# Output biases of a routed feed-forward layer: from a matrix product at the end to rows gathered per expert and added at the evacuation

## The chip, the core and the metric

The kernel runs on one core of a Trainium2 chip. Times are device microseconds (us) of one execution on that core. Engines: PE is TensorE's matmul, PEld its weight load, DVE is VectorE, ACT is ScalarE, POOL is GpSimd, SP is SyncE, which only issues transfers here. POOL issues every indirect transfer (rows picked by a list of numbers) and some plain ones.

## What is computed

There are 625 tokens of width 1024. A layer norm and a relational graph convolution come first (20000 edges, two kinds, 286 hidden columns, ELU, product with `wo`), then a second layer norm and a feed-forward part with two shared experts and two of eight routed experts for each token:

```python
sh = gelu(einsum('td,sdh->sth', xf, sW1) + sb1)          # 2 shared experts
shared = (einsum('sth,shd->std', sh, sW2) + sb2).mean(0)
topk_vals, topk_idx = top_k(xf @ rW + rb, 2)
probs = softmax(topk_vals)                               # two weights that sum to 1
y = einsum('eth,ehd->etd', gelu(einsum('td,edh->eth', xf, W1) + b1), W2) + b2
out = x + shared + sum over the two chosen experts of probs * y
```

The change concerns the two biases of the second products, `sb2` (2 x 1024) and `b2` (8 x 1024).

## The kernel before

Tokens lie in NT = 5 tiles of TP = 125. The kernel is one straight program, `sparse_kernel`; a framework puts each engine's instructions in an order and adds the waits, and a tile of a pool is handed out again when its last user is through. `tc.issue_after(x)` places an instruction behind `x`. A second, dense kernel stands behind a flag and is not entered here.

The stages, in order of PE:

1. Counting and projection (up to 88 us). Edges become one-hot columns `ohs` and `ohk` on DVE (the last instruction on `ohs` is L850), PE counts them (`cnt`), and between these it forms the projections `p_pr` (L891). POOL starts with constants and small loads, among them those of `bd`, a DRAM table of both biases three times over (L625, L627).
2. Aggregation and output product of the graph part (`p_agg`, `p_y`, up to 134 us), with the second layer norm; rows of the norm go to DRAM as `h2d`, those of the residual as `x1d`.
3. Routing (134 to 170 us). `gate` forms the gates, `route` the two weights `w`, `slots` gives every token-expert pair a place. There are NJ = 11 routed tiles of 128 places; a tile is one expert's, or is shared by two of 64 places or four of 32. In `slots` DVE makes one-hots `oh` and `oj` (L1242 to L1246), a product of them on PE gives `p_tok` (L1250), and DVE reads from it `tok` (which token a place holds) and `row` (where in DRAM its result goes). PE fills the time with the shared experts' first product, `shared_in` (`p_sh`, L1137), whose calls are written out between these steps. Then `weights_T` splits the weights into three bfloat16 parts, transposes them on PE (`p_wT`, L1298) into `wT`, and `bias_parts` loads `bd` three times into `b2x` (L635) and splits it into `b23` (L639, L640, L642).
4. Routed experts, first product (170 to 221 us). `fetch` gathers the tokens of a tile from `h2d` into a tile `xs` of the pool `io`, which has three buffers (L1332); PE transposes them (`p_x`), multiplies (`p_h`, L1359) and transposes back (`p_hT`).
5. Routed experts, second product (221 to 260 us). For every tile of `ORDER` PE makes two halves `p_yj` of 128x512 (L1417) in five PSUM banks; the halves are copied to a tile `ys` of the pool `gat` (15 buffers of 4 KB a partition) by DVE (L1421), from the fifth tile on every first half by ACT (L1423). POOL then scatters the 128 rows to the DRAM table `yt` (L1425). `gat` also holds copies `w2m` of weights for the shared tiles (12 of them, made by ACT, L1408) and later the gathered rows `gs`.
6. Output (260 us to the end). PE makes the shared experts' second product `p_o`: for each of 11 column groups eight float32 matmuls (L1472), and one of bfloat16, `wT` against `b23`, which adds all biases (L1474). SP loads the result rows of both choices of each token, `gs`, from `yt` (L1436) once the scatters have landed. DVE adds in a fixed order (L1448): half of `p_o` to `x1` for a group, and each `gs` times its weight; the rows of the last three token tiles are added in one block ahead of their `p_o`. Then the output is stored.

The place the biases have in this:

```python
                nc.tensor.matmul(p[:TP, :n], wT[:, own], b23[:, at], start=False, stop=True)
            add(x1[:, d, at], p[:TP, :n], 1.0 / NS, x1[:, d, at])
```

Of the kernel before, what the change touches and what calls it, by code (L numbers as in the profile page):

```python
# [8 lines left out]
F32 = mybir.dt.float32  # L9
# [8 lines left out]
N = 625  # L18
# [434 lines left out]
def sparse_kernel(  # L453
# [166 lines left out]
    for i in (2, 3):  # L620
        nc.gpsimd.tensor_add(join, join, ident[:, QC * i : QC * (i + 1)])


    bd = dram.tile([3, NS + NE, D], F32, name="bd")
    nc.gpsimd.dma_start(bd[:, :NS, :], bass.AP(tensor=sb2.tensor, offset=sb2.offset,  # L625
                                               ap=[[0, 3], [D, NS], [1, D]]))
    nc.gpsimd.dma_start(bd[:, NS:, :], bass.AP(tensor=b2.tensor, offset=b2.offset,  # L627
                                               ap=[[0, 3], [D, NE], [1, D]]))
    b23 = const.tile([3 * QC, D], BF16, name="b23")

    def bias_parts():
        b2x = io.tile([3 * QC, D], F32, tag="io", name="b2x")
        nc.vector.memset(b2x, 0.0)
        for j in range(3):
            nc.gpsimd.dma_start(b2x[j * QC : j * QC + 3 * (NS + NE)], bd.rearrange("i e d -> (i e) d"))  # L635
        b2h = rt.tile([3 * QC, D], BF16, name="b2h")
        for j in range(3):
            with tc.issue_after(named.ins):
                nc.vector.tensor_copy(b2h, b2x)  # L639
            nc.scalar.copy(b23[j * QC : (j + 1) * QC], b2h[j * QC : (j + 1) * QC])  # L640
            if j < 2:
                nc.vector.tensor_sub(b2x, b2x, b2h)  # L642

# [180 lines left out]
    nc.vector.memset(nil, 0.0)  # L824
    MAXG = max(GROUPS)
    ends = [R * TP * min(DB * (b + 1), NT) for b in range((NT + DB - 1) // DB)]

    def count_windows(between):
        accs = []
        c0 = 0  # L830
        for g in GROUPS:
# [17 lines left out]
            nc.vector.tensor_tensor(os, row[:, None].to_broadcast(shape), key, op=ALU.is_equal)  # L849
            nc.vector.tensor_tensor(os, os, both(VV_, 128)[1], op=ALU.mult)  # L850
            shape, key = both(KW_, KR)
# [148 lines left out]
    at(50, clear)  # L1000
    at(30, transpose_vec)
    at(6, scales, 0, 2)
    at(18, scales, 2, 4)
# [93 lines left out]
    w = const.tile([TP, NT, NS + NE], F32, name="w")  # L1097
    wT = hid.tile([3 * QC, N], BF16, name="wT")
    sel = const.tile([TP, NT, NE], F16, name="sel")
    wide = [TP, NT, NE]  # L1100

    def route():
        full = [TP, NT, NE, NE]
        other = gates[:, :, None, :].to_broadcast(full)
        own = gates[:, :, :, None].to_broadcast(full)
        nc.vector.tensor_scalar(lower, lower, 0.0, None, op0=ALU.is_gt)
        above = rt.tile(full, F32, name="above")
        equal = rt.tile(full, F32, name="equal")
        nc.vector.tensor_tensor(above, other, own, op=ALU.is_gt)
        nc.vector.tensor_tensor(equal, other, own, op=ALU.is_equal)  # L1110
        nc.vector.tensor_mul(equal, equal, lower[:, None, :, :].to_broadcast(full))
        nc.vector.tensor_add(above, above, equal)
        cnt = const.tile(wide, F32, name="cnt")
        nc.vector.tensor_reduce(cnt, above, axis=AX.X, op=ALU.add)
        nc.vector.tensor_scalar(sel, cnt, 1.5, None, op0=ALU.is_lt)
        top = const.tile([TP, NT], F32, name="top")
        nc.vector.tensor_reduce(top, gates, axis=AX.X, op=ALU.max)
        ex = const.tile(wide, F32, name="ex")
        nc.vector.tensor_sub(ex, gates, top[:, :, None].to_broadcast(wide))
        nc.scalar.activation(ex, ex, AF.Exp)  # L1120
        nc.vector.tensor_mul(ex, ex, sel)
        tot = const.tile([TP, NT], F32, name="tot")
        nc.vector.tensor_reduce(tot, ex, axis=AX.X, op=ALU.add)
        inv = const.tile([TP, NT], F32, name="tot_inv")
        nc.vector.reciprocal(inv, tot)
        nc.vector.memset(w[:, :, :NS], 1.0)
        nc.vector.tensor_mul(w[:, :, NS:], ex, inv[:, :, None].to_broadcast(wide))
# [18 lines left out]
    tok = const.tile([128, NJ], I32, name="tok")  # L1146
    row = const.tile([128, NJ], I32, name="row")
    ej = const.tile([1, nt + 4], I32, name="ej")

    def slots():  # L1150
# [64 lines left out]
        both_ = [TP, 2, NT, NE]  # L1215
        nc.vector.tensor_tensor(m, m, ab[:, :, :, None].to_broadcast(both_), op=ALU.is_equal)
        nc.vector.tensor_mul(m, m, w[:, None, :, NS:].to_broadcast(both_))
        nc.vector.tensor_reduce(wab, m, axis=AX.X, op=ALU.add)
# [19 lines left out]
        oh = rt.tile([TP, 2, NT, 128], F16, name="oh")  # L1238
        oj = const.tile([TP, 2, NT, NJ], F16, name="oj")
        q = ps_mm("p_tok")  # L1240
        for a in range(2):
            nc.vector.tensor_tensor(oh[:, a], it[:, None, :].to_broadcast([TP, NT, 128]),  # L1242
                                    pc[:, 0, a][:, :, None].to_broadcast([TP, NT, 128]), op=ALU.is_equal)
            nc.vector.tensor_tensor(oj[:, a], it[:, None, :NJ].to_broadcast([TP, NT, NJ]),
                                    pc[:, 1, a][:, :, None].to_broadcast([TP, NT, NJ]), op=ALU.is_equal)
            nc.vector.tensor_mul(oj[:, a], oj[:, a], tid[:, a, :, None].to_broadcast([TP, NT, NJ]))  # L1246
        shared_in(0, 1)
        for a in range(2):
            for t in range(NT):
                nc.tensor.matmul(q[:, :NJ], oh[:, a, t], oj[:, a, t],  # L1250
                                 start=(a == 0 and t == 0), stop=(a == 1 and t == NT - 1))
# [3 lines left out]
        nc.vector.scalar_tensor_tensor(t[:, 1], q[:, :NJ], -1.0, t[:, 0], op0=ALU.add, op1=ALU.subtract)  # L1255
        named = nc.vector.tensor_scalar(tok, t[:, 1], 0.0, float(N - 1), op0=ALU.max, op1=ALU.min)
        nc.vector.tensor_scalar(t[:, 0], q[:, :NJ], 0.5, 4.0 * YB, op0=ALU.is_lt, op1=ALU.mult)
        nc.vector.tensor_tensor(row, t[:, 0], q[:, :NJ], op=ALU.add)

        for at in (0, NH2):  # L1260
# [18 lines left out]
        nc.vector.tensor_tensor(flag, flagf[:, 0:1], flagf[:, 1:2], op=ALU.add)  # L1279
        return named  # L1280

    def weights_T():
        nc.vector.tensor_scalar(w[:, :, NS:], w[:, :, NS:], float(NS), None, op0=ALU.mult)
        NW_ = NS + NE
        part = rt.tile([TP, NT, 3 * QC], F32, name="part")
        nc.vector.memset(part, 0.0)
        near = const.tile([TP, NT, NW_], BF16, name="near")
        for i in range(3):
            nc.vector.tensor_copy(near, w)
            for j in range(3):  # L1290
                at = j * QC + i * NW_
                nc.vector.tensor_copy(part[:, :, at : at + NW_], near)
            if i < 2:
                nc.vector.tensor_sub(w, w, near)
        for a, b in ((0, 3), (3, NT)):
            p = ps_mm(f"p_wT_{a}")
            for d in range(a, b):
                nc.tensor.transpose(p[: 3 * QC, (d - a) * TP : (d - a + 1) * TP], part[:, d, :],  # L1298
                                    ident[:TP, :TP])
            nc.vector.tensor_copy(wT[:, a * TP : b * TP], p[: 3 * QC, : (b - a) * TP])  # L1300

    gate()
    route()
    named = slots()
    weights_T()
    bias_parts()
    for t in range(HK):
# [92 lines left out]
    gat = pool(ctx, "gat", 15, side="right")  # L1400

    ORDER = (*whole[:3], *range(NM2), *whole[3:])
    w2m = {}
    for j in ORDER:
        for a, _, e in parts(j)[1:]:
            for k in range(HK):
                w2m[j, a, k] = gat.tile([128, D], F32, tag="y", name=f"w2m_{j}_{a}_{k}")
                nc.scalar.copy(w2m[j, a, k][:, None, :], w2a[:, bass.ds(e, 1), k, :])  # L1408
    sent = []
    for n, j in enumerate(ORDER):  # L1410
        y = gat.tile([128, D], F32, tag="y", name=f"ys_{j}")
        for s in range(2):
            at = slice(s * 512, (s + 1) * 512)
            p = ps_acc(f"p_yj_{j}_{s}")
            for k in range(HK):
                for a, b, e in parts(j):
                    made = nc.tensor.matmul(p[a:b], hjT[:, j, k, a:b],  # L1417
                                     w2m[j, a, k][:, at] if a else w2a[:, bass.ds(e, 1), k, at],
                                     start=(k == 0), stop=(k == HK - 1))
            if s or n < 4:  # L1420
                nc.vector.tensor_copy(y[:, at], p)  # L1421
            else:
                nc.scalar.copy(y[:, at], p)  # L1423

        sent.append(nc.gpsimd.indirect_dma_start(  # L1425
            out=yt, out_offset=bass.IndirectOffsetOnAxis(ap=row[:, j : j + 1], axis=0), in_=y, in_offset=None,
            bounds_check=2 * YB - 1, oob_is_err=False))
        for s in sent[:-1]:
            tc.declare_no_dep(sent[-1].ins, s.ins, reason="rows of different slots")

    gs = {}
# [27 lines left out]
    for d in range(NT):  # L1459
# [4 lines left out]
        for at in ((0, 512), (512, D)) if d < NT - 1 else ((0, 512), (512, 768), (768, D)):  # L1464
# [4 lines left out]
            with tc.issue_after(made.ins):  # L1469
                for i in range(NS):  # L1470
                    for k in range(HK):
                        nc.tensor.matmul(p[:TP, :n], shT[:, i, k, own], sw2[:, i, k, at],  # L1472
                                         start=(i == 0 and k == 0), stop=False)
                nc.tensor.matmul(p[:TP, :n], wT[:, own], b23[:, at], start=False, stop=True)  # L1474
            add(x1[:, d, at], p[:TP, :n], 1.0 / NS, x1[:, d, at])
# [47 lines left out]
```

## Time and profile before

| what | us |
|---|---|
| median of 3 runs (lowest, highest) | 304.88 (304.16, 305.06) |
| the profiled execution, its own time | 303.7 |
| its span in the trace | 301.4 |
| PE busy | 290.8 (96%) |
| DVE busy | 168.4 (56%) |
| ACT busy | 107.5 (36%) |
| POOL busy | 45.2 (15%) |

The trace covers 301.4 us of an execution that took 303.7 us; the 2.3 us around it belong to start and end. The granted TensorE clock was 0.997 of full speed. Sums made from the trace are differences against 301.4 or 303.7, and the same difference is then set against the median. A row of the groups gives busy time, mean nanoseconds of one instruction, and the idle time before it with what ended it; the chain gives, in order of time, the start, the length, the engine and the line of each piece of work that set the end.

### The profile page before, as it was taken

What the parts mean: (1) busy time and instruction counts of PE and PEld (TensorE: products, weight loads), DVE (VectorE), ACT (ScalarE), POOL (GpSimd) and SP (SyncE); (2) the same over time, 40 slices, a digit from 0 to 9 for tenths busy, and PEclk for the clock granted to TensorE, in tenths of its full rate; (3) what the DMA queues carried; (4) which work ended last, traced back from release to release, by engine and by line L of the source; (5) the groups of instructions that cost most, each with busy time, mean ns of one, the idle gap of its engine ahead of it and who ended that gap; (6) DMA issues with size and microseconds to landing.
All of it is one profiled execution on the core that took longest, in us unless ns stands there. A gap on an engine that the chain in (4) does not pass through costs nothing.

```text
span 301.4 us, 4682 instructions
## 1 busy us (share of the span) xinstructions
PE 290.8 (96%) x1649; PEld 194.9 (65%) x1649; DVE 168.4 (56%) x465; ACT 107.5 (36%) x246; POOL 45.2 (15%) x98
## 2 busy tenths in 40 slices
PE   8799999999999799999999999999999999999993
PEld 6687777787889534376777887887843334444452
DVE  5999999998327668756883122212223211255921
ACT  2455118355334432155123244638359311000000
POOL 9500000000000014240131212210003222200000
PEclk9999999999999999999999999999999999999998
DMA  7999910000009999965999253340057555479442
GB/s 243 304 318 393 421 65 2 0 2 1 0 17 340 348 348 391 400 195 182 348 396 410 86 203 96 114 141 3 0 190 276 221 209 210 191 291 385 161 138 73
DMA packets 27408, 61.15 MB, mean 203 GB/s; under 512 B 2176, under 2 KB 16007, under 8 KB 27375
## 3 DMA queue, kind: packets, MB, share of 16 engines
q1 hardware_dynamic: 21806, 43.77, 40.7%
q0 software_dynamic: 5280, 16.69, 15.7%
q10 hardware_dynamic: 294, 0.35, 0.5%
q8 instruction: 15, 0.25, 0.3%
q14 instruction: 13, 0.10, 0.1%
HBM read 42.76 MB, written 18.81 MB: 204 GB/s over the span
## 4 chain that ended last, share of the span: by engine, by line
PE 93%; DVE 4%; ACT 1%; issue 0%; ACTq 0%
PE p_pr L891 20%; PE p_h L1359 13%; PE p_yj L1417 13%; PE p_o L1472 11%; PE p_sh L1137 10%; PE p_y L952 6%; PE p_agg L909 6%; PE p_x L1340 3%; PE p_t L795 3%; PE cnt L868 2%; PE p_y L956 2%; PE p_hT L1371 1%; PE scrap L972 1%; PE p_gate L1085 1%; PE p_o L1474 1%; DVE ln_4s L727 0%
## 5 line engine op out<-in xcount | busy, mean ns | idle before, releaser
L891 PE MATMUL p_pr<-wg,nT 128*125 128x286 f32 x240 | 62.5, 409 | 0.0
L891 PEld LDWEIGHTS p_pr<-wg,nT 128*125 128x125 f32 x240 | 43.2, 187 | 11.3 <-ACT nT L801 0.2
L1359 PE MATMUL p_h<-w1a,xsT 128*128 (+2 forms) x176 | 40.0, 380 | 0.0
L1417 PE MATMUL p_yj<-w2a,hjT 128*128 (+2 forms) x88 | 38.6, 594 | 0.0
L1472 PE MATMUL p_o<-sw,shT 128*125 128x512 f32 (+1 forms) x88 | 36.1, 553 | 0.0
L1137 PE MATMUL p_sh<-h2T,sw 128*128 128x313 f32 (+1 forms) x128 | 35.2, 428 | 0.0
L1359 PEld LDWEIGHTS p_h<-w1a,xsT 128*128 128x128 f32 (+2 forms) x176 | 28.7, 168 | 7.4 <-issue 0.5
L1137 PEld LDWEIGHTS p_sh<-h2T,sw 128*128 128x128 f32 x128 | 23.6, 189 | 8.6 <-issue 0.2
L1417 PEld LDWEIGHTS p_yj<-w2a,hjT 128*128 128x128 f32 (+2 forms) x88 | 14.4, 168 | 22.4 <-issue 22.4
L1472 PEld LDWEIGHTS p_o<-sw,shT 128*125 128x125 f32 x88 | 16.4, 187 | 16.9 <-issue 16.2
L1421 DVE COPY ys<-p_yj 128x512 f32<-128x512 f32 x15 | 10.4, 692 | 28.7 <-PE p_yj L1417 26.5
L1363 DVE COPY hj<-p_h 128x256 f32<-128x256 f32 x11 | 4.7, 425 | 30.8 <-PE p_h L1359 30.8
L909 PE MATMUL p_agg<-P,CT 125*125 125x287 bf16 x150 | 20.1, 287 | 1.6 <-DVE agg L915 1.6
L966 POOL DMA_DIRECT2D x1d<-xh x10 | 5.3, 532 | 98.5 <-DVE xh L959 98.5
L909 PEld LDWEIGHTS <-CT 125*125 125x125 bf16 x150 | 18.5, 136 | 2.5 <-issue 2.0
L1425 POOL DMA_INDIRECT yt<-ys,row x11 | 10.8, 984 | 50.5 <-DVE ys L1421 50.5
L952 PE MATMUL p_y<-wo_t,eT 128*125 128x512 f32 x40 | 18.1, 595 | 0.0
L1332 POOL DMA_INDIRECT xs<-h2d,tok x11 | 11.2, 1015 | 45.0 <-PE p_x L1340 30.9
L1374 ACT ACTIVATE hjT<-p_hT,vT 128x128 f32<-128x128 f32 (+2 forms) x34 | 8.7, 332 | 24.5 <-PE p_hT L1371 24.5
L1344 DVE COPY xsT<-p_x 128x512 f32<-128x512 f32 x11 | 7.6, 692 | 17.4 <-PE p_x L1340 13.8
L1448 DVE SCALAR_TENSOR_TENSOR x<-p_o,x 125x512 f32<-125x512 f32 (+1 forms) x11 | 6.9, 641 | 16.3 <-PE p_o L1474 16.3
L1359 PE MATMUL p_h<-w1m,xsT 128*64 128x256 f32 (+1 forms) x96 | 14.7, 381 | 0.0
(302 smaller groups left out, 424.0 us busy)
## 6 DMA issues: line engine op xcount, KB each, us to landing
w1a<-in_L_ffn_W_dram SPq DMA_DIRECT2D x8, 1024.0 KB, 10.5
w2a<-in_L_ffn_W_dram SPq DMA_DIRECT2D x8, 1024.0 KB, 4.8
yt<-zero SPq DMA_DIRECT2D x2, 2560.0 KB
g<-yt SPq DMA_DIRECT2D x10, 512.0 KB, 6.7
sw<-in_L_ffn_sW_dram SPq DMA_DIRECT2D x4, 1024.0 KB, 5.0
x<-x1d SPq DMA_DIRECT2D x5, 500.0 KB
wg<-in_L_gnn_W_rel_dram SPq DMA_DIRECT2D x2, 1144.0 KB, 19.1
x1d<-xh POOLq DMA_DIRECT2D x5, 448.0 KB, 6.7
```

The lines of the kernel that those rows point to most:

```text
L795: nc.tensor.transpose(pv[:, k, :], row[:, at : at + 128], ident[:TP, :TP])
L891: nc.tensor.matmul(p[:TP, :F], nT[:, k, m * TP : (m + 1) * TP], wg[:, k, r, :], start=(k == 0), stop=(k == KD - 1))
L909: nc.tensor.matmul(p[:TP, : F + 1], CT[:, m, at : at + TP], P[:, m, r, i], start=(m == 0 and i == 0), stop=(m == NT - 1 and i == 2))
L952: nc.tensor.matmul(ps[s][:TP, :], eT[:, k, :], wo_t[:, k, s * 512 : (s + 1) * 512], start=(k == 0), stop=False)
L1137: nc.tensor.matmul(p[:, : z - a], sw1[:, i, k, t * 128 : (t + 1) * 128], h2T[:, k, a:z], start=(k == 0), stop=(k == KD - 1))
L1332: nc.gpsimd.indirect_dma_start(out=xs, out_offset=None, in_=h2d, in_offset=bass.IndirectOffsetOnAxis(ap=tok[:, j : j + 1], axis=0))
L1340: nc.tensor.transpose(p[:, k * 128 : (k + 1) * 128], xs[:, at : at + 128], ident)
L1359: nc.tensor.matmul(p[a:b, :H], xsT[j][:, k, a:b], w1m[j, a][:, 0, k, :] if a else w1a[:, bass.ds(e, 1), k, :], start=(k == 0), stop=(k == ...
L1417: made = nc.tensor.matmul(p[a:b], hjT[:, j, k, a:b], w2m[j, a, k][:, at] if a else w2a[:, bass.ds(e, 1), k, at], start=(k == 0), stop=(k = ...
L1421: nc.vector.tensor_copy(y[:, at], p)
L1425: sent.append(nc.gpsimd.indirect_dma_start(out=yt, out_offset=bass.IndirectOffsetOnAxis(ap=row[:, j : j + 1], axis=0), in_=y, in_offset=No ...
L1472: nc.tensor.matmul(p[:TP, :n], shT[:, i, k, own], sw2[:, i, k, at], start=(i == 0 and k == 0), stop=False)
```

## The change

The biases leave the product at the end. Since a token's two weights sum to 1, `b2` of an expert plus the mean of both `sb2` can be added to every result row of that expert before it is weighted.

- At the start POOL loads the biases into a small SBUF tile `b2p` (three loads of 128 runs of 256 bytes) in place of the two loads of `bd`. Behind the last one-hots of the counting stage DVE forms the sums (two instructions of 128x64), and POOL writes them to DRAM as `b2d`, eight rows of 1024.
- `slots` also finds the expert of each place: a product and a sum on DVE, a second set of columns in `oj` (two more products), `p_tok` with 22 columns in place of 11, and one more instruction that reads `es_` from it.
- `weights_T` and `bias_parts` go, with `wT`, `b23`, `b2x` and `bd`; so does the matmul of L1474.
- In the second product each `ys` tile is first filled by an indirect load of 128 rows of `b2d` (`fetch_bias`), four tiles ahead: the first three in `io`, the others in `gat`. DVE adds both halves of `p_yj` to it; ACT copies none. POOL's order is four bias loads, then in turn a scatter and a bias load, then the last scatters alone.

```diff
-    bd = dram.tile([3, NS + NE, D], F32, name="bd")
...
+    b2d = dram.tile([NE, D], F32, name="b2d")
+    BC = 128 // NE
+    b2p = fbig.tile([128, NS + 1, D // BC], F32, name="b2p")
+    for i, v in enumerate((sb2[0], sb2[1], b2)):
+        of = v.offset
+        ap = [[D // BC, 128], [1, D // BC]] if i == NS else [[0, NE], [D // BC, BC], [1, D // BC]]
+        nc.gpsimd.dma_start(b2p[:, i], bass.AP(tensor=v.tensor, offset=of, ap=ap))
+
+    def bias_rows():
+        for i in range(NS):
+            with tc.issue_after(hot[-1].ins):
+                nc.vector.scalar_tensor_tensor(b2p[:, NS], b2p[:, i], 1.0 / NS, b2p[:, NS], op0=ALU.mult, op1=ALU.add)
+        nc.gpsimd.dma_start(b2d.rearrange("e (c w) -> (e c) w", c=BC), b2p[:, NS])
...
+    at(EC - 1, bias_rows)
...
+        nc.vector.tensor_tensor(me.rearrange("p a t e -> p (a t) e"), m.rearrange("p a t e -> p (a t) e"),
+                                it[:, None, :NE].to_broadcast([TP, 2 * NT, NE]), op=ALU.mult)
...
+            nc.vector.tensor_reduce(expert, me, axis=AX.X, op=ALU.add)
...
-            nc.vector.tensor_mul(oj[:, a], oj[:, a], tid[:, a, :, None].to_broadcast([TP, NT, NJ]))
+            nc.vector.tensor_mul(o1, o0, expert[:, a, :, None].to_broadcast([TP, NT, NJ]))
+            nc.vector.tensor_mul(o0, o0, tid[:, a, :, None].to_broadcast([TP, NT, NJ]))
...
+        nc.vector.tensor_scalar(es_, q[:, NJ : 2 * NJ], float(NE - 1), None, op0=ALU.min)
...
-    weights_T()
-    bias_parts()
...
+    def fetch_bias(n):
+        ys[n] = (io.tile([128, D], F32, tag="io", name=f"ys_{n}") if n < 3
+                 else gat.tile([128, D], F32, tag="y", name=f"ys_{n}"))
+        j = ORDER[n]
+        fetched.append(nc.gpsimd.indirect_dma_start(
+            out=ys[n], out_offset=None, in_=b2d, in_offset=bass.IndirectOffsetOnAxis(ap=es_[:, j : j + 1], axis=0)))
+
+    for n in range(AHEAD):
+        fetch_bias(n)
...
-            if s or n < 4:
-                nc.vector.tensor_copy(y[:, at], p)
-            else:
-                nc.scalar.copy(y[:, at], p)
+            nc.vector.tensor_tensor(y[:, at], p, y[:, at], op=ALU.add)
...
+        if n + AHEAD < NJ:
+            fetch_bias(n + AHEAD)
...
-                nc.tensor.matmul(p[:TP, :n], wT[:, own], b23[:, at], start=False, stop=True)
```

More of the change, by code (lines that the diff above doesn't have):

```diff
@@ L621, in sparse_kernel @@
         nc.gpsimd.tensor_add(join, join, ident[:, QC * i : QC * (i + 1)])
-    bd = dram.tile([3, NS + NE, D], F32, name="bd")
[L625 to L642, printed above, removed]
+    b2d = dram.tile([NE, D], F32, name="b2d")
[10 more added lines that the diff above has]
+        nc.gpsimd.dma_start(b2d.rearrange("e (c w) -> (e c) w", c=BC), b2p[:, NS])
     rw_t = const.tile([128, KD, QC], F32, name="rw_t")
@@ L825, in sparse_kernel @@
     MAXG = max(GROUPS)
+    hot = []
     ends = [R * TP * min(DB * (b + 1), NT) for b in range((NT + DB - 1) // DB)]
@@ L849, in count_windows @@
             nc.vector.tensor_tensor(os, row[:, None].to_broadcast(shape), key, op=ALU.is_equal)
-            nc.vector.tensor_tensor(os, os, both(VV_, 128)[1], op=ALU.mult)
+            hot.append(nc.vector.tensor_tensor(os, os, both(VV_, 128)[1], op=ALU.mult))
             shape, key = both(KW_, KR)
@@ L1097, in sparse_kernel @@
     w = const.tile([TP, NT, NS + NE], F32, name="w")
-    wT = hid.tile([3 * QC, N], BF16, name="wT")
     sel = const.tile([TP, NT, NE], F16, name="sel")
@@ L1125, in route @@
         nc.vector.reciprocal(inv, tot)
-        nc.vector.memset(w[:, :, :NS], 1.0)
         nc.vector.tensor_mul(w[:, :, NS:], ex, inv[:, :, None].to_broadcast(wide))
@@ L1147, in sparse_kernel @@
     row = const.tile([128, NJ], I32, name="row")
+    es_ = const.tile([128, NJ], I32, name="es_")
     ej = const.tile([1, nt + 4], I32, name="ej")
@@ L1216, in slots @@
         nc.vector.tensor_tensor(m, m, ab[:, :, :, None].to_broadcast(both_), op=ALU.is_equal)
+        expert = const.tile([TP, 2, NT], F16, name="expert")
+        me = const.tile([TP, 2, NT, NE], F16, name="me")
+        nc.vector.tensor_tensor(me.rearrange("p a t e -> p (a t) e"), m.rearrange("p a t e -> p (a t) e"),
+                                it[:, None, :NE].to_broadcast([TP, 2 * NT, NE]), op=ALU.mult)
         nc.vector.tensor_mul(m, m, w[:, None, :, NS:].to_broadcast(both_))
@@ L1238, in slots @@
         oh = rt.tile([TP, 2, NT, 128], F16, name="oh")
-        oj = const.tile([TP, 2, NT, NJ], F16, name="oj")
+        oj = const.tile([TP, 2, NT, 2, NJ], F16, name="oj")
+        with nc.allow_low_precision("whole numbers up to 7"):
+            nc.vector.tensor_reduce(expert, me, axis=AX.X, op=ALU.add)
         q = ps_mm("p_tok")
@@ L1243, in slots @@
                                     pc[:, 0, a][:, :, None].to_broadcast([TP, NT, 128]), op=ALU.is_equal)
-            nc.vector.tensor_tensor(oj[:, a], it[:, None, :NJ].to_broadcast([TP, NT, NJ]),
+            o0, o1 = (oj[:, a, :, i] for i in range(2))
+            nc.vector.tensor_tensor(o0, it[:, None, :NJ].to_broadcast([TP, NT, NJ]),
                                     pc[:, 1, a][:, :, None].to_broadcast([TP, NT, NJ]), op=ALU.is_equal)
-            nc.vector.tensor_mul(oj[:, a], oj[:, a], tid[:, a, :, None].to_broadcast([TP, NT, NJ]))
+            nc.vector.tensor_mul(o1, o0, expert[:, a, :, None].to_broadcast([TP, NT, NJ]))
+            nc.vector.tensor_mul(o0, o0, tid[:, a, :, None].to_broadcast([TP, NT, NJ]))
         shared_in(0, 1)
@@ L1249, in slots @@
             for t in range(NT):
-                nc.tensor.matmul(q[:, :NJ], oh[:, a, t], oj[:, a, t],
+                nc.tensor.matmul(q[:, : 2 * NJ], oh[:, a, t], oj[:, a, t].rearrange("p i j -> p (i j)"),
                                  start=(a == 0 and t == 0), stop=(a == 1 and t == NT - 1))
@@ L1255, in slots @@
         nc.vector.scalar_tensor_tensor(t[:, 1], q[:, :NJ], -1.0, t[:, 0], op0=ALU.add, op1=ALU.subtract)
-        named = nc.vector.tensor_scalar(tok, t[:, 1], 0.0, float(N - 1), op0=ALU.max, op1=ALU.min)
+        nc.vector.tensor_scalar(tok, t[:, 1], 0.0, float(N - 1), op0=ALU.max, op1=ALU.min)
         nc.vector.tensor_scalar(t[:, 0], q[:, :NJ], 0.5, 4.0 * YB, op0=ALU.is_lt, op1=ALU.mult)
         nc.vector.tensor_tensor(row, t[:, 0], q[:, :NJ], op=ALU.add)
+        nc.vector.tensor_scalar(es_, q[:, NJ : 2 * NJ], float(NE - 1), None, op0=ALU.min)
         for at in (0, NH2):
@@ L1279, in slots @@
         nc.vector.tensor_tensor(flag, flagf[:, 0:1], flagf[:, 1:2], op=ALU.add)
[L1280 to L1300, printed above, removed]
     gate()
     route()
-    named = slots()
-    weights_T()
-    bias_parts()
+    slots()
     for t in range(HK):
@@ L1400, in sparse_kernel @@
     gat = pool(ctx, "gat", 15, side="right")
+    AHEAD = 4
     ORDER = (*whole[:3], *range(NM2), *whole[3:])
@@ L1408, in sparse_kernel @@
                 nc.scalar.copy(w2m[j, a, k][:, None, :], w2a[:, bass.ds(e, 1), k, :])
-    sent = []
+    sent, fetched, ys = [], [], {}
+    def fetch_bias(n):
[6 more added lines that the diff above has]
+        fetch_bias(n)
     for n, j in enumerate(ORDER):
-        y = gat.tile([128, D], F32, tag="y", name=f"ys_{j}")
+        y = ys[n]
         for s in range(2):
@@ L1419, in sparse_kernel @@
                                      start=(k == 0), stop=(k == HK - 1))
-            if s or n < 4:
-                nc.vector.tensor_copy(y[:, at], p)
-            else:
-                nc.scalar.copy(y[:, at], p)
-        sent.append(nc.gpsimd.indirect_dma_start(
-            out=yt, out_offset=bass.IndirectOffsetOnAxis(ap=row[:, j : j + 1], axis=0), in_=y, in_offset=None,
-            bounds_check=2 * YB - 1, oob_is_err=False))
+            nc.vector.tensor_tensor(y[:, at], p, y[:, at], op=ALU.add)
+        with tc.issue_after(fetched[-1].ins):
+            sent.append(nc.gpsimd.indirect_dma_start(
+                out=yt, out_offset=bass.IndirectOffsetOnAxis(ap=row[:, j : j + 1], axis=0), in_=y, in_offset=None,
+                bounds_check=2 * YB - 1, oob_is_err=False))
         for s in sent[:-1]:
             tc.declare_no_dep(sent[-1].ins, s.ins, reason="rows of different slots")
+        if n + AHEAD < NJ:
+            fetch_bias(n + AHEAD)
     gs = {}
@@ L1472, in sparse_kernel @@
                         nc.tensor.matmul(p[:TP, :n], shT[:, i, k, own], sw2[:, i, k, at],
-                                         start=(i == 0 and k == 0), stop=False)
-                nc.tensor.matmul(p[:TP, :n], wT[:, own], b23[:, at], start=False, stop=True)
+                                         start=(i == 0 and k == 0), stop=(i == NS - 1 and k == HK - 1))
             add(x1[:, d, at], p[:TP, :n], 1.0 / NS, x1[:, d, at])
```

## The prediction

> **What bounds the kernel now.** I read the chain of work that ended last, first by engine, then in order of time, to see which removed instruction lies on it.
>
> ```profile
> PE 93%; DVE 4%; ACT 1%; issue 0%; ACTq 0%
> ```
>
> ```profile
> 152.49 0.24 PE p_tok L1250 x10
> 152.73 4.32 PE p_sh L1137 x16
> 157.04 0.54 PE p_wT L1298 x5
> 157.58 12.62 PE p_sh L1137 x48
> ...
> 259.66 3.43 PE p_o L1472 x8
> 263.10 0.22 PE p_o L1474
> 263.32 3.44 PE p_o L1472 x8
> ...
> 296.11 0.13 PE p_o L1474
> 296.26 0.42 DVE x L1448
> ```
>
> From 133.5 us to 296.2 us the chain never leaves PE, piece on piece: PE is the bound here, and work taken from it is time gained as long as nothing else becomes late. The five transposes of `p_wT` and the eleven matmuls of L1474 are on it. Next, the groups of the page and the times to landing, for the engines that take over the work:
>
> ```profile
> L1421 DVE COPY ys<-p_yj 128x512 f32<-128x512 f32 x15 | 10.4, 692 | 28.7 <-PE p_yj L1417 26.5
> L1425 POOL DMA_INDIRECT yt<-ys,row x11 | 10.8, 984 | 50.5 <-DVE ys L1421 50.5
> xs<-h2d,tok POOLq DMA_INDIRECT x11, 4.4
> yt<-ys,row POOLq DMA_INDIRECT x11, 7.3
> ```
>
> DVE and POOL wait for PE in the second product. A 512 KB gather lands 4.4 us after its issue at the median (4.0 to 9.5), a scatter after 7.3 (3.2 to 8.6). Last, windows of the second product (columns: stretch, length, then busy time and count of PE, PEld, DVE, ACT, POOL, the clock, the DMA share, GB/s) and DVE's timeline at the two places where DVE comes close to PE:
>
> ```profile
> 221.00:230.00 9.00, 9.00 (x25) 4.17 (x24) 3.11 (x5) 8.26 (x17) 1.74 (x2) 1.00 0.83 300
> 230.00:240.00 10.00, 10.00 (x44) 3.35 (x45) 3.46 (x5) 5.95 (x7) 2.25 (x3) 1.00 0.58 232
> 240.00:250.00 10.00, 10.00 (x54) 3.38 (x49) 1.98 (x3) 1.76 (x3) 2.93 (x3) 1.00 0.50 203
> 250.00:260.00 10.00, 10.00 (x25) 4.43 (x24) 1.77 (x4) 1.76 (x3) 2.93 (x3) 1.00 0.53 211
> ```
>
> ```profile
> 152.08 0.20 DVE L1246 TENSOR_TENSOR oj<-oj,tid 125x55 f16<-125x55 f16 x1
> 275.04 10.16 DVE L1448 SCALAR_TENSOR_TENSOR x<-g,wab,x 125x1024 f32<-125x1024 f32 x8
> 288.93 0.69 DVE L1448 SCALAR_TENSOR_TENSOR x<-p_o,x 125x512 f32<-125x512 f32 x1 [1.94 <-PE p_o L1474]
> ```
>
> The last input of `p_tok` is ready at 152.28 us and PE's first matmul of it starts at 152.33: no margin there. At the end, DVE is behind PE for the block of eight row additions and has caught up at 287.
>
> **What the Trainium skill says.** "TensorE: Matmul & The Clock Gate" (section "Wait — 56ns, not 53.3ns?") prices a warm bfloat16 matmul of 512 columns at 215.7 ns from start to start; the chain's 0.22 agrees. "VectorE: DVE Perf Modes" ("Why PSUM operands drop a tier") has float32 from PSUM at one element a cycle for copy and two-operand alike; here the copy takes 692 ns, and the addition of PSUM to SBUF in the graph part (L959, 125x512) 684, so it agrees. "SBUF — State Buffer" ("Who interferes with whom") says that a Vector instruction with only one SBUF input outside the two-port modes does not hold up POOL; the new addition is one, and no trace yet shows it beside bias loads. "DMA: Bandwidth & Descriptors" ("Issuing engines are not separate DMA queues") has all queues share 16 engines; the gathers' 9.5 us in a stage that loads weights at 321 GB/s fit that.
>
> **The change, part by part.**
>
> *L1474 goes.* Nine steps of 0.217 us (263.10 to 263.32), one of 0.11, one of 0.13: 2.19 us, all on the chain. The eight float32 steps of a group keep 0.43 each.
>
> *weights_T and bias_parts go.* `p_wT` gives 0.54 us on the chain. The DVE and ACT work (8 us of DVE between 152 and 161, three ACT copies) lies beside `p_sh`; DVE then idles 10.25 us until 171, so it is worth nothing. Three POOL loads of `b2x` at 143 us go; the first gather is set by `tok`, not by them. The third gather, which waited until 161.19 for `b2h`, may go about 5 us earlier beside the weight loads; the first two still have from 155 to 170 to land: 0.
>
> *slots grows.* Four instructions are put ahead of the last `oj`: the product `me` (0.15 us from start to start, as L1217), its sum (0.15, as L1218), two products on `oj` (0.12 each, as L1246). Two tiny ones trade places. `oj` is ready 0.54 us later. PE works in order and has only `p_sh` L1137 behind `p_tok`, so this is a new stall. PE takes the second half's `oj` some 0.12 us after its first matmul: I take a loss of 0.45. Ends: 0.2 (DVE's gaps swallow part) and 0.9 (each new instruction at its full 0.2). The ten wider `p_tok` matmuls (22 columns for 11) and `es_` cost under 0.1 us. `tok` and the first gather move by the same 0.45, with the gather done well before 170.
>
> *The front.* POOL's two bias loads become three, and `rw_t` goes out about 0.6 us later; it is needed at 134. 96 KB in 384 runs replace 120 KB read and written; the graph weights loaded beside it (until some 31 us) are first needed at 37. The two DVE sums stand where a memset of `part` stood (458 ns at 73.2): about 0.4 us by L1191's rows, no difference. `b2d` is written by about 80 us, when POOL and DMA idle; the next user of its SBUF, the load of `w1a`, starts at about 90. All 0, at worst 0.3 either way.
>
> *Evacuation.* 22 additions at 0.69 us are 15.2 us of DVE in 38; one half comes every 1.72 us (the copies start at 226.60, 228.32, 230.03). ACT's copies go, DVE still waits for PE: 0.
>
> *Bias loads.* Eleven of 512 KB, about 1 us of POOL each. The first three use `io`, free when the last `p_x` are done, at about 204, 209 and 214, with DMA idle. The fourth needs memory that `p_h` frees at 221, and is wanted at 233.5. Later ones go out behind a scatter: the 5th at 226.9 (wanted 237.2), the 6th at 230.3 (240.5), the 7th at 234.4, when the fourth tile's matmuls free its buffer (244.1), the last at about 248 (258.0). So each has 9.7 us or more. Behind a waiting bias load on POOL is the next scatter, which isn't due before 236. Behind a waiting addition on DVE is the next half, and PE only stalls once five banks are full, about 6 us later. Traffic from 230 to 250 grows from 0.54 by some 0.39 share (three loads, 1.57 MB, per 10 us at about 405 GB/s for full share) to 0.93. I expect landings of 6 to 10 us: hidden, 0. Below, nothing can be gained; above, see the rival.
>
> *The tail.* No bias load is issued after 248, so the last scatter (261.1) should land in its 3.3 us as before and SP's loads of `gs` follow at 264. The buffers of `gs` are all free by then. DVE has 1.94 us of idle time at 287, then 2.96 and 1.15: with PE's groups 0.22 shorter, row additions may come about 5 us late before they set the end.
>
> Sum: 2.19 + 0.54 - 0.45 = **2.28 us** off PE's chain. The profiled execution would go from 301.4 to 299.1 (its time from 303.7 to 301.4); against the median of 304.88 it is **302.6**.
>
> **Rivals.**
>
> *A, the stall at `p_tok` is larger and a little of the tail shows.* With 0.9 lost there and 0.5 at the front or tail: gain 1.3, 303.6. For it: DVE is busy without a gap from 144 to 153. Against: the counted instructions are few. It belongs to the likely case's range.
>
> *B, the end moves to DVE's row additions.* If crowded scatters put the last landing 6 to 7 us later, the additions use up the 5 us and most of the gain: 304.2 to 305. For it: a scatter took 8.6 us even before. Against: the crowding ends ten microseconds before the last scatter.
>
> *C, slower: bias loads set the pace of the second product.* A bias load goes out about 1.2 us after the addition four tiles back, so if it takes L to land, the 7th is late by L - 9.7 and the 11th, issued behind the 7th's scatter, by as much again plus L - 10.1: together 2L - 19.8. Banks and tail take 5.5. The gain is gone from L = 14; at L = 17 the loss is 14.2 - 5.5 - 2.3 = 6.4: 311. For it: the 128 rows come from eight rows of DRAM, which no transfer of before does in this size (the broadcast of `cb`, 140 KB from one row, took 6.7 us), and they share a queue with the scatters. Against: under a full DMA the slowest gather took 9.5.
>
> *D, the removed matmuls are no time on PE.* Excluded by the chain, which goes from group to group in 3.655 us with the short one and 3.43 without.
>
> **How the numbers follow.** A measurement of this kernel tells about 0.3% (0.9 us) from no change. Main case with A: 0.79 (302.6; A's share 0.15); B: 0.11; C: 0.10. Below 303.97 is the main case and A: 0.79 faster; B is same, 0.11; C slower, 0.10. The range starts at 301.7 (nothing lost at `p_tok`, 0.4 of run-to-run spread) and reaches to 304.7 over A and most of B; C is left out.
>
> **What would show it.** In the changed profile: no L1474, groups of `p_o` 3.43 us apart; no `p_wT`; PE idle of 0.2 to 0.9 us before `p_tok`, ended by DVE `oj`; additions of about 690 ns waiting for PE, not for a DMA; bias loads landing in under 10 us; the last scatter at about 261. An addition that waits for a bias load with PE idle behind it in 235 to 260 us would make it wrong (C), and so would a last stretch in which DVE's additions wait for `gs` and PE doesn't set the end (B).

## The result: no gain, a little slower, and the profile after

The changed kernel takes 306.35 us at the median (305.26 to 308.22) beside 304.88 of the kernel before. The ratio is 1.0053, 95% interval 1.0028 to 1.0078: slower by half a per cent, where 302.6 and a gain were forecast. (A ratio compares the fast runs of a kernel with those of the kernel before that were taken beside them; the latter's median was 305.5 us for experiments 1, 2, 3 and 6 and 304.44 for 4 and 5, so a ratio is not a quotient with 304.88.) The profiled executions took 306.48 against 303.7 us, their spans are 304.7 and 301.4. These two differ by more than the medians do, 3.3 us of span against 1.5, since the profiled execution of the kernel before was a quick one: the traces tell where time went, the medians how much.

The chain by engine, and the group of the new additions, from the page of the changed kernel:

```profile
PE 71%; DMA 14%; DVE 7%; issue 3%; POOL 1%; SPq 1%; ACT 1%; POOLq 0%; DVEq 0%; ACTq 0%
L1413 DVE TENSOR_TENSOR ys<-p_yj,ys 128x512 f32<-128x512 f32 x22 | 14.7, 689 | 33.8 <-DMA ys<-b2d,es__1591 20.3
```

PE's share of the chain fell from 93% to 71%. Not all of this is the change's: of the 14% DMA, 4% is a load of `x` in the first 17 us, which both kernels have. But a transfer that the kernel before doesn't have, the bias load, holds DVE up for 20.3 us in all. The chain in order of time (start, length, what) shows where:

```profile
153.27 0.14 DVE oj L1249
153.45 0.27 PE p_tok L1253 x5
...
227.65 10.52 DMA ys<-b2d,es__1591
...
241.52 18.33 DMA ys<-b2d,es__1591
259.97 0.70 DVE ys L1413
260.71 1.98 PE p_yj L1410 x4
262.70 34.41 PE p_o L1465 x88
297.13 0.42 DVE x L1441
```

Two bias loads of 10.5 and 18.3 us (from the start of their issue) stand in the middle of the second product. The waits from 221 us to the end (in all, times, longest) have the rest of the path, from the load over DVE to PE, and a second place near the end:

```profile
DVE ys L1413 <- DMA ys<-b2d,es__1591: 20.3, 6, 4.1
DVE x L1441 <- DMA g<-yt: 8.0, 5, 6.5
PEld p_yj L1410 <- DVE ys L1413: 4.8, 4, 2.5
```

Set against each other by stage, from the starts in both chains:

| stage | before | after | difference |
|---|---|---|---|
| start to the last `p_t` before routing | 133.47 | 134.08 | +0.61 |
| routing, to `p_x` | 36.74 | 36.58 | -0.16 |
| both expert products, to `p_o` | 89.45 | 92.04 | +2.59 |
| `p_o`, to the last addition | 36.60 | 34.43 | -2.17 |
| last addition to the end of the span | 5.1 | 7.6 | +2.4 |

The gain of the last product is there; the second expert product and the tail give back twice as much. In the second product the additions from the sixth tile on come at a pace that isn't PE's. DVE's timeline (start, length, what, in brackets the idle time before; the profile puts the third of these waits to "issue", but that tile's load, issued at 238.24, landed 16.2 us later, just before it):

```profile
243.94 1.29 DVE L1413 TENSOR_TENSOR ys<-p_yj,ys 128x512 f32<-128x512 f32 x2 [4.02 <-DMA ys<-b2d,es__1591]
249.20 1.29 DVE L1413 TENSOR_TENSOR ys<-p_yj,ys 128x512 f32<-128x512 f32 x2 [3.96 <-DMA ys<-b2d,es__1591]
254.57 1.29 DVE L1413 TENSOR_TENSOR ys<-p_yj,ys 128x512 f32<-128x512 f32 x2 [4.09 <-issue]
259.97 1.29 DVE L1413 TENSOR_TENSOR ys<-p_yj,ys 128x512 f32<-128x512 f32 x2 [4.11 <-DMA ys<-b2d,es__1591]
265.17 1.29 DVE L1413 TENSOR_TENSOR ys<-p_yj,ys 128x512 f32<-128x512 f32 x2 [3.91 <-DMA ys<-b2d,es__1591]
```

One tile every 5.2 to 5.4 us, where PE needs 3.4. The times from issue to landing:

```profile
ys<-b2d,es__1591 POOLq DMA_INDIRECT x11, 12.8
yt<-ys,row POOLq DMA_INDIRECT x11, 13.5
```

Bias loads land after 12.8 us at the median (4.0 to 18.2), and the scatters, which the change leaves as they are, need 13.5 in place of 7.3. So something slows every indirect transfer. The sum of the traffic doesn't explain it: from about 244 us on the DMA share is mostly well under one. The share in 40 slices of 236 to 270 us, and the GB/s of each, first for the kernel before, then for the changed one:

```profile
DMA  3386334943395336333884379315900650369999
GB/s 135 130 347 280 135 125 193 366 164 130 159 386 217 130 125 270 149 125 125 328 347 159 130 308 371 121 58 231 386 0 0 265 227 0 58 207 419 424 371 424
```

```profile
DMA  8799999969733979823659853693333496333396
GB/s 352 241 342 352 395 357 294 390 231 386 251 135 154 381 270 386 251 106 130 260 164 299 318 169 125 246 429 135 130 135 140 178 405 231 135 125 135 145 395 275
```

Both fall again and again to a floor, a lowest value that keeps coming back: share 0.3 and about 130 GB/s. In the kernel before the floor goes away at about 258 us, and the share then drops to 0 between transfers; in the changed kernel it lasts to about 269. A steady 0.3 fits five of sixteen engines (0.31) at work and eleven idle. One transfer of this stretch has a shape for that: the load of `x1`, five tiles of 125 partitions. **The Trainium skill**, "DMA: Bandwidth & Descriptors" (section "Why a DMA increments its semaphore by 16 and not by 1"), has a transfer use the largest number of engines up to 16 that divides the slowest dimension of both its sides; 125 is divided by 5. Its section "Queues, rings and completion order" has each engine alternate between the queues that have work for it. Whether this case agrees is what the experiments below ask.

From this comes **theory E**, five engines. At 130 GB/s over five engines a packet of 4 KB takes 0.158 us (the trace's packets: 0.159). The rest is an estimate from these figures. From 221 us on, each of the five has the second shared weights (2 MB over 16 engines, 5.1 us), `x1` (125 packets, 19.9) and 8 rows of each of 11 scatters (14.0): 39 us of work, to 260, about as long as PE's second product. The change adds 8 rows of each of the 8 bias loads issued from then on, 10.2 us: to 270. A bias load is complete when its slowest eight rows are, so the five full engines would hold up all. A scatter and a bias load take each engine 2.5 us; alternating with `x1` that is about 5.1, the pace seen. The rivals: **P**, POOL's queue needs 2.6 us for each indirect transfer, two to a tile; **R**, the bias loads read 128 rows out of only eight rows of DRAM; **B**, the bandwidth of the whole is full.

### The profile page after: what moved, and what is told of

Same layout as the page of the kernel before. It is cut to its first block, busy times and chain, and to the rows that moved or that the text cites. A ratio compares the mean times of both kernels' runs of the same rounds, so it can differ in the third digit from the quotient of the medians.

```text
span 304.7 us, 4650 instructions
## 1 busy us (share of the span) xinstructions
PE 289.1 (95%) x1633; PEld 192.9 (63%) x1633; DVE 165.6 (54%) x454; ACT 100.4 (33%) x236; POOL 55.0 (18%) x108
## 4 chain that ended last, share of the span: by engine, by line
PE 71%; DMA 14%; DVE 7%; issue 3%; POOL 1%; SPq 1%; ACT 1%; POOLq 0%; DVEq 0%; ACTq 0%
PE p_pr L886 17%; PE p_h L1340 13%; PE p_o L1465 11%; DMA ys<-b2d,es__1591 9%; PE p_sh L1131 8%; PE p_y L947 6%; PE p_agg L904 6%; DMA xh<-in_x_dram 4%; PE p_x L1321 3%; PE p_y L951 2%; PE p_t L789 2%; PE cnt L863 1%; DVE st L751 1%; PE p_hT L1352 1%; PE p_gate L1081 1%
## 5 line engine op out<-in xcount | busy, mean ns | idle before, releaser
L1465 PE MATMUL p_o<-sw,shT 128*125 128x512 f32 (+1 forms) x88 | 34.6, 554 | 0.0
L1340 PEld LDWEIGHTS p_h<-w1a,xsT 128*128 128x128 f32 (+2 forms) x176 | 28.7, 168 | 7.4 <-issue 0.5
L1413 DVE TENSOR_TENSOR ys<-p_yj,ys 128x512 f32<-128x512 f32 x22 | 14.7, 689 | 33.8 <-DMA ys<-b2d,es__1591 20.3
L1410 PEld LDWEIGHTS p_yj<-w2a,hjT 128*128 128x128 f32 (+2 forms) x88 | 14.2, 168 | 25.2 <-issue 20.3
L1313 POOL DMA_INDIRECT xs<-h2d,tok x11 | 10.4, 947 | 55.1 <-PE p_x L1321 34.8
L1441 DVE SCALAR_TENSOR_TENSOR x<-g,wab,x 125x1024 f32<-125x1024 f32 x10 | 12.8, 1284 | 8.1 <-DMA g<-yt 8.0
L1398 POOL DMA_INDIRECT ys<-b2d,es__1591 x11 | 10.5, 956 | 21.3 <-PE p_x L1321 11.1
```

What stands on the lines that cost most here:

```text
L1313: nc.gpsimd.indirect_dma_start(out=xs, out_offset=None, in_=h2d, in_offset=bass.IndirectOffsetOnAxis(ap=tok[:, j : j + 1], axis=0))
L1340: nc.tensor.matmul(p[a:b, :H], xsT[j][:, k, a:b], w1m[j, a][:, 0, k, :] if a else w1a[:, bass.ds(e, 1), k, :], start=(k == 0), stop=(k == ...
L1398: fetched.append(nc.gpsimd.indirect_dma_start(out=ys[n], out_offset=None, in_=b2d, in_offset=bass.IndirectOffsetOnAxis(ap=es_[:, j : j + 1 ...
L1410: made = nc.tensor.matmul(p[a:b], hjT[:, j, k, a:b], w2m[j, a, k][:, at] if a else w2a[:, bass.ds(e, 1), k, at], start=(k == 0), stop=(k = ...
L1413: nc.vector.tensor_tensor(y[:, at], p, y[:, at], op=ALU.add)
L1441: added.append(nc.vector.scalar_tensor_tensor(*args, op0=ALU.mult, op1=ALU.add))
```

## The experiments

**1. The load of `x1` over 128 partitions, in the changed kernel.** The first four tiles load 128 rows (the last three unused), the last is split in 112 and 13; the additions take the first 125 partitions.

```diff
-    x1 = late.tile([TP, NT, D], F32, name="x1")
-    for t in range(NT):
-        nc.sync.dma_start(x1[:, t, :], x1d[t * TP : (t + 1) * TP, :])
+    x1 = late.tile([128, NT, D], F32, name="x1")
+    for t in range(NT - 1):
+        nc.sync.dma_start(x1[:, t, :], x1d[t * TP : t * TP + 128, :])
+    for g in PARTS:
+        nc.sync.dma_start(x1[g, NT - 1, :], x1d[(NT - 1) * TP + g.start : (NT - 1) * TP + g.stop, :])
```

> The changed kernel, with the loads of x1 over 128 partitions in place of 125 (the last tile as 112 + 13 rows); the rows past 125 are overwritten by nothing and read by nobody. Theory E (five engines): a load of 125 partitions is spread over only five of the sixteen DMA engines, since 125 rows divide into 16 equal parts no better than into 5; these five carry x1 and their share of every scatter and bias load until about 261 us, and that sets the 5.2 us from addition to addition. Then with x1 on all sixteen: bias loads land in at most 8 us at the median (12.8 in the changed kernel), additions of the tiles 5 to 10 about 3.4 us apart, p_o starts near 260.0 (262.7 in the changed kernel), and the time is 302.0 to 303.3, faster than before. Rival P (POOL's software queue needs 2.6 us for each indirect transfer, two per tile): the pace stays 5.2 us, p_o starts at 262 to 263, time 305.5 to 306.5. Rival R (a bias load reads 128 rows out of eight rows of DRAM): as P, no change. Rival B (DMA as a whole is full): bytes are the same, no change.

Measured: 301.5 us, ratio to the kernel before 0.9878 (0.9847 to 0.991). The chain, by engine from its page, then in order of time:

```profile
PE 90%; DVE 7%; ACT 1%; issue 0%; ACTq 0%
```

```profile
133.57 1.04 PE p_t L789 x8
...
222.22 37.40 PE p_yj L1412 x134
259.62 34.37 PE p_o L1467 x88
294.01 0.42 DVE x L1443
```

PE runs through the second product in 37.40 us, as in the kernel before:

```profile
222.27 37.40 PE p_yj L1417 x134
```

The share from 236 to 270 us has lost its floor:

```profile
DMA  9999999999999999999996694029202810479989
GB/s 400 424 400 424 289 304 323 390 419 424 415 410 429 410 424 390 415 381 371 381 342 265 241 414 193 29 111 414 92 0 111 333 58 0 106 279 381 390 294 357
```

Nearly the same bytes (12 rows of 4 KB more) now go at full share until about 254, then come single transfers with 0 between. The landings and the additions of the sixth and seventh tile:

```profile
ys<-b2d,es__1591 POOLq DMA_INDIRECT x11, 8.4
yt<-ys,row POOLq DMA_INDIRECT x11, 6.5
243.75 1.29 DVE L1415 TENSOR_TENSOR ys<-p_yj,ys 128x512 f32<-128x512 f32 x2 [4.33 <-DMA ys<-b2d,es__1591]
246.25 1.29 DVE L1415 TENSOR_TENSOR ys<-p_yj,ys 128x512 f32<-128x512 f32 x2 [1.21 <-DMA ys<-b2d,es__1591]
```

This speaks against B: from 240 to 260 us the share is 0.90 (0.71 in the changed kernel), and PE is busy throughout. It speaks against R, whose cause is untouched, and against P: two indirect transfers to a tile go through here every 2.5 us. The expectation was off in three points. The time is below its range of 302.0 to 303.3. Bias loads land after 8.4 us at the median, not in at most 8. And the sixth tile's additions start as late as in the changed kernel, at 243.75, DVE having waited 4.33 us for the load; but the next follow 2.5 us apart, and PE's banks cover it.

**2. The same edit in the kernel before.**

> The kernel before with the same edit of the x1 loads as the last run. Theory E: scatters land in 3 to 5 us at the median (7.3 before), but PE sets the pace there, so the time stays within 0.5 us of before, perhaps a few tenths better at the end. Rivals P, R and B: scatter landings and time as before. Tells whether what the last run gains belongs to the change or to x1 alone.

Measured: 304.85 us, ratio 0.9982 (0.9965 to 0.9999). The scatters now land in

```profile
yt<-ys,row POOLq DMA_INDIRECT x11, 3.3
```

in place of 7.3 us, which P, R and B don't give. The time is 0.18% less, 0.55 us, a little over the half us that was allowed. So the five engines were crowded before the change as well; it cost little, since PE never waited for a scatter. The layout of `x1` is worth at most 0.35% there, and 1.7% (0.9878 against 1.0053) in the changed kernel.

**3. Other rows, in the changed kernel.** It then adds token rows where the biases were, and leaves the biases out.

```diff
-            out=ys[n], out_offset=None, in_=b2d, in_offset=bass.IndirectOffsetOnAxis(ap=es_[:, j : j + 1], axis=0)))
+            out=ys[n], out_offset=None, in_=h2d, in_offset=bass.IndirectOffsetOnAxis(ap=tok[:, j : j + 1], axis=0)))
```

> The changed kernel, with each bias load gathering the tile's token rows of h2d (128 different rows) in place of its bias rows of b2d (at most eight different rows); result rows so get token rows added instead of biases. Rival R (hot rows of DRAM): landings fall to 4 to 8 us, pace 3.4 us, time about 302.6. Theory E, rivals P and B: landings stay at 12 to 13 us at the median, pace 5.2 us, time 305.5 to 307.

Measured: 306.23 us, ratio 1.0034 (1.0014 to 1.0053). The landings:

```profile
ys<-h2d,tok POOLq DMA_INDIRECT x11, 12.9
yt<-ys,row POOLq DMA_INDIRECT x11, 13.5
```

128 different rows land just as late as 128 out of eight, and the additions again follow 5.1 to 5.4 us apart up to the last but one. R falls.

**4. The same 125 rows in parts of 112 and 13, in the changed kernel.** This leaves rows, bytes and the tile as they are, and changes only what the partitions divide by.

```diff
     for t in range(NT):
-        nc.sync.dma_start(x1[:, t, :], x1d[t * TP : (t + 1) * TP, :])
+        for g in PARTS:
+            nc.sync.dma_start(x1[g, t, :], x1d[t * TP + g.start : t * TP + g.stop, :])
```

> The changed kernel, with each load of x1 in two parts of 112 and 13 partitions: the same 125 rows and bytes as in the changed kernel, twice the loads. Theory E (the number of DMA engines that a load is spread over is the largest up to 16 that divides its partitions: 16 for 112, 13 for 13, 5 for 125): as with 128 partitions, p_o starts near 260.0, time 301.3 to 302.5. If instead the 128 partitions helped in some other way (whole rows of the tile, other SBUF addresses), the pace stays at 5.2 us and the time at 306.

Measured: 301.81 us, ratio 0.9907 (0.9873 to 0.9941). The second product again takes PE 37.40 us; `p_o` starts at 261.31 and not near 260, because this execution reached `p_t` 1.7 us later than the first experiment. Bias loads land after 8.9 us at the median, and from the start of `p_t` (135.27) to that of the last addition (295.70) it is 160.43 us, against 160.44 in the first experiment.

**5. Parts of 122 and 3: the dose.** The edit of the last run with `(slice(0, 122), slice(122, TP))` for `PARTS`.

> The changed kernel, with each load of x1 in two parts of 122 and 3 partitions: the same rows, bytes and number of loads as in the last run. Theory E: 122 divides by 2 and by no larger number up to 16, so two engines carry 61 rows of each of five tiles, 305 x 0.159 = 48.5 us, in place of 19.9 us on each of five; with 19 scatters and bias loads (24 us) and sw2 (5 us) they are full until about 299 us, and the loads of gs queue behind x1 on them. The pace stays at 5.2 us to the last tile, the first row addition on gs comes some 20 us late, and the time is 315 to 325. If the number of engines is not what matters, it is as the last run or as the changed kernel: 301 to 307.

Measured: 333.88 us, ratio 1.0952 (1.0915 to 1.099). The share from 270 to 331 us:

```profile
DMA  3511111111114999999211138688999500589820
GB/s 140 199 54 54 54 54 51 54 51 51 54 51 97 301 263 333 236 266 242 64 51 51 54 81 344 234 317 322 408 330 322 220 38 0 118 279 255 273 98 0
```

The floor is now 51 to 54 GB/s at a share of 0.1: two engines of sixteen (0.125), each with the 26 GB/s of before. So both counts, 5 for 125 and 2 for 122, are those of the rule from which theory E was made. The additions again follow 5.1 to 5.3 us apart up to the last but one, as expected: by the theory each of the two, like each of the five, has the rows of `x1` to alternate with those of the indirect transfers. The chain in order of time shows what the expectation had too small:

```profile
261.81 1.69 SPq L1381
263.55 14.20 SPq L1381
...
278.88 8.66 SPq L1381
287.70 18.93 DMA g<-yt
306.73 1.29 DVE x L1442
```

SP stands at the loads of `x1` (L1381) until 287.5, although the last scatter had landed at 278.4, so `gs` is issued only at 287.7 and lands at 306.7. What SP waits for there the trace doesn't name. The first row addition comes 28.7 us later than in the changed kernel (278.0), where some 20 was expected, and ten row additions of 1.28 us and the `p_o` additions then queue up on DVE, another 18 us to the last of them. The direction and the number of engines are E's; the size of the loss was not foreseen.

**6. `p_tok` waits less, on top of the first experiment.** The DVE instructions of `slots` that only the weight loads need go behind the last product on `oj`:

```diff
-            nc.vector.tensor_mul(o0, o0, tid[:, a, :, None].to_broadcast([TP, NT, NJ]))
+            ready = nc.vector.tensor_mul(o0, o0, tid[:, a, :, None].to_broadcast([TP, NT, NJ]))
...
+        with tc.issue_after(ready.ins):
...
```

> The first run's kernel, and in slots the DVE instructions that only the loads of weights need (kt, ge, es, gq, ej, flag) are put behind the last product on oj, which p_tok waits for. Expected under each theory: p_tok waits 0.4 us less, so the time is 0.3 to 0.5 us under the first run's; against it, the weight loads of the experts are issued about 2 us later, which costs nothing if their first user starts at 170 as before.

Measured: 301.07 us, ratio 0.9858 (0.9829 to 0.9887), the best of all here. The chain passes `p_tok` without DVE:

```profile
144.64 8.52 PE p_sh L1131 x32
153.17 0.24 PE p_tok L1253 x10
153.41 16.93 PE p_sh L1131 x64
170.34 1.75 PE p_x L1322 x16
```

From `p_t` (134.15) to `p_x` it is 36.19 us, against 36.58 in the changed kernel and in the first experiment: 0.39 less. The times agree in size (0.4), but their intervals overlap, so the trace carries this point.

## Why the prediction was wrong

*Wrong: the bias loads, put at "hidden, 0".* The failed step is the sum of the traffic, "from 0.54 by some 0.39 share" to 0.93, from which landings of 6 to 10 us followed. It took the mean share of sixteen engines as the fill of each. The window rows of 0.50 and 0.53 that the prediction showed were a mixture: 0.53 of sixteen is the work of 8.5 engines, and if five of them were full, the other eleven shared 3.5, a third each. On the five there was no room for 0.39. Hence landings of 12.8 us at the median and 18.2 at most. POOL issues a bias load behind the scatter of the tile four before it, and that scatter waits for its own tile's addition; so one late load makes a later one late, and the stage took 2.59 us longer. With `x1` on all engines the share from 240 to 260 us is 0.90, close to the sum, and PE waits for none of the loads: the sum was right for all sixteen together and wrong for the five. A sign was there: scatters of 7.3 us at a mean share of 0.5, which the prediction took for general crowding. With `x1` spread they are 3.3.

*Wrong: the tail, put at 0.* It was to stay as it was because the last scatter would go out at 261.1. That scatter waits for the last addition, which waits for the last bias load, and it went out 9.4 us late; first the kernel before, then the changed one:

```profile
261.14 0.98 POOL L1425 DMA_INDIRECT yt<-ys,row  x1 [2.39 <-DVE ys L1421]
270.56 0.97 POOL L1416 DMA_INDIRECT yt<-ys,row  x1 [2.84 <-DVE ys L1413]
```

SP's first load of `gs` was issued at 274.3 in place of 264.5, the first row addition started at 278.0 in place of 268.1, and DVE waited 8.0 us for `gs`. The prediction had allowed 5 us before late row additions would show. SP's stores then began at 285.5 in place of 273.3, and the end of the span moved 2.4 us further from the last addition. In the first experiment the last scatter goes out at 260.6, DVE waits once for `gs`, 0.95 us, and the last addition ends 4.6 us before the end of the span, as before (4.7).

*Rival C, given 0.10, is what happened: bias loads set the pace.* The cause it named for slow loads, the eight rows of DRAM, is excluded by the third experiment; the queue shared with the scatters is how the delay passes on. Its rule held. The loads of the 7th and the 11th tile landed after

```profile
ys<-b2d,es__1591 POOLq DMA_INDIRECT x1, 13.4
ys<-b2d,es__1591 POOLq DMA_INDIRECT x1, 16.8
```

which by the rule makes the last tile (13.4 - 9.7) + (16.8 - 10.1) = 10.4 us late; its addition starts at 268.99, against 257.99 in the first experiment, of which 0.5 is the front. Less the 5.5 us that banks and tail were to take, 4.9 us of loss remain; the table has 2.59 + 2.4 = 5.0. So close an agreement is luck in part, as the landings differ from load to load. What C lacked was a reason for such landings: the shape of a transfer that the change doesn't touch.

*Right: the last product and the routing.* L1474 was to give 2.19 us and gave 2.17. `p_wT` and the stall at `p_tok` were to make -0.54 + 0.45; the stage measured -0.16, so the stall is 0.38, and the sixth experiment, which takes 0.39 out, shows its cause. *Right: the evacuation on DVE*, 689 ns each, hidden where the loads come in time. *The front, put at 0, is not decided.* With the front of the kernel before, two traces reach `p_t` at 133.47 and 134.30 us; with the changed front, six reach it between 133.57 and 135.64. The 0.61 of the table lies within this spread, and a loss of some tenths there would not be seen.

Without the crowded engines the sum holds. From `p_t` to the start of the last addition the kernel before takes 162.79 us, with the `x1` edit or without; the first experiment takes 160.44: -2.35, forecast -2.28. The ratio of that run, 0.9878, is a somewhat larger gain than 2.35 of 303.7 (0.9923) and the 0.9982 of the `x1` edit make together (0.9905). That product lies inside its interval; whether more than noise is left there stays open.

## What to carry to other kernels

Before traffic is added to a stage, look at the share in fine slices and not at its mean: a floor that repeats (0.3 here, 0.1 with two engines) was the sign of a transfer that used only a part of the engines, and transfers spread over all of them landed late with it (scatters after 7.3 us, 3.3 without). Check what each load's partitions divide by; 125 as 112 and 13 doubled the number of these loads and was worth 1.5% here (0.9907 against 1.0053). Such a load may cost nothing until a change makes something wait, so a change that fails may need a repair elsewhere rather than to be undone.

## What the runs showed that was not expected

- Where a load of 125 partitions set the floor, 125 to 135 GB/s moved, where one of 122 did, only 51 to 54: about 26 GB/s for each of five or two engines.
- Gathering 128 rows out of eight was no slower than 128 different rows: 12.8 and 12.9 us under load, and the first three bias loads, at an idle DMA, landed in 4.0 to 4.6 us, beside 4.4 for the token gathers at the median.
- With loads on two engines, SP stood at single loads of its queue for 14 and 16 us, and the loads behind them were issued only afterwards.
